# A two-layer graph attention kernel: where the second layer's tiles live and are cleared, how the first layer's last groups are drained, and how the last four norms are ordered

## The chip, the core and the metric

The kernel runs on one core of a Trainium2 chip. Its engines work side by side, each through its own instructions in the order written: PE (matmul; weight loads, PEld, run beside it), DVE (vector), ACT (scalar functions and copies), POOL (GpSimd, which also issues the gathers) and SP (here only a queue for transfers). The metric is device time in microseconds, lower is better. Time before: 877.46 us, the median of three runs (876.76 to 881.76).

## The reference

Eight graphs share one adjacency of 2048 nodes. x is (8, 2048, 64).

```
mask = adj + eye(N) > 0
h   = einsum('bnc,hdc->bhnd', x, Wh)                  # 4 heads of 64
out = softmax(where(mask, h h^T, -1e16)) h + bh
z   = leaky_relu(concat over heads, 0.2)
h2  = einsum('bnk,dk->bnd', z, Wo)
z2  = leaky_relu(softmax(where(mask, h2 h2^T, -1e16)) h2 + bo, 0.2)
y   = (z2 - mean) * rsqrt(var + 1e-5) * gamma + beta
result = layernorm(x + y)
```

So each node passes two norms at the end: the layer's own (with gamma and beta), then, after the residual, a second one.

## The kernel before, in words

The adjacency is sparse but for 56 dense "hub" nodes. The other 1992 nodes are put in 166 sets of 12. For each set the program lists at most 128 neighbours, and a gather on POOL (L792) fetches their rows for all eight graphs, 260 KB, from a table in memory: table1 holds x, table2 holds the first layer's output.

Tiles come from pools. `const` lives through the whole program. `early`, `rowp` and `work` serve the first layer and are released together after it. `late` is opened after that and serves the second layer, in the same memory. The order of instructions on each engine is the order in which the program writes them.

**First layer.** A loop over i from -4 to 85 works on groups of two sets (83 groups). In iteration i, in program order: scores of group i+1 on PE and their mask on DVE (L826); projection of group i-1 on PE into a PSUM tile `cat` (tag C, two banks), copied by ACT (L518, z); ACT copies xTg and takes the exponential; values of group i on PE, reciprocal and scaling on DVE (L853, L854, osb); two gathers; DVE's leaky step (L523); then for group i-2 the second layer's map on PE (L880) into `cat`, for group i-3 a transpose (L890) into `cat`; columns of i+4 into `cat`; DVE copies the map (L885, own) and adds the bias to the transposed rows (L894, rowt), which two transfers on SP store to table2 (L897); picking jobs on DVE; ACT's copy y (L812) and, after PE's transposes, its copy otb (L870), which the next projection needs. PSUM tags S, T, O and C have one buffer each, so a new tile of a tag waits for the readers of the last one. The last iterations (83 to 85) only drain groups.

**Between the layers** the first 24 gathers from table2 are issued on POOL, and DVE clears the tiles of the second layer (L1107 to L1117): `ownb` (the hubs' own columns, block-wise), three `bd` (the sets' own columns, block-wise, refilled by ACT in `spread_own`, L1124), two `es2` (weights), two `esh` (hub weights), and `linked` (a byte mask). They are `late` tiles.

**Second layer.** A loop over steps u from -4 to 48 takes four sets a step (42 steps with sets): scores of u+2 (PE, exponential on ACT), values of u, gathers of u+6, hub blocks for some steps, `roots(u)` (logarithm and exponential on ACT, which make 1/sqrt of the variances gathered in a batch), `spread_own(u+3)`, transposed scores of u+1 and their mask on DVE (L1152), transposes of u+4 with ACT copies (L1320). Every second step ends a block of 8 sets, and `norm` hands back its jobs, which are laid into later steps: for a norm that begins in step v, each step has a first and a second slot.

- v, second slot: scale by the softmax sum, leaky step, row sums (L1186 to L1197)
- v+1, first: centre on DVE (L1202), square on ACT (L1204)
- v+2, first: variance on DVE (L1213), into a batch whose root is taken in step v+2
- v+3, second: scale (L1217), times gamma (L1221), plus residual xr (L1222), row sums
- v+4, first: centre, square; v+6, first: variance; v+7, first: scale and store

Eight transfers store a norm's rows (L1248), all on SP, but for the last norm, where four go on the ACT queue. There are 21 such norms (v = 1, 3, ... 41) and one for the hubs.

Of the kernel before, what the change touches and what calls it, by code (L numbers as in the profile page):

```python
# [359 lines left out]
def fast_kernel(ctx: ExitStack, tc: tile.TileContext, x, adj, Wh, bh, Wo, bo, gamma, beta, out, flag):  # L360
# [51 lines left out]
    make_identity(nc, ident)  # L412
    identb = const.tile([P, P], BF16, name="identb")
    nc.vector.tensor_copy(identb, ident)
    wnat = early.tile([P, H, C], F32, name="wnat")
    whT = early.tile([P, H * D], F32, name="whT")
    gram = early.tile([P, H, P], F32, name="gram")
    wos = early.tile([D, H * D], F32, name="wos")
# [68 lines left out]
    number = early.tile([P, 2, HALFN], U16, name="number")  # L487
# [81 lines left out]
    yh = early.tile([P, 2, 2 * HUB * H], F32, name="yh")  # L569

    def hub_columns():
        py = two("pyh")
# [87 lines left out]
    hub_osb = {}  # L660


    keys = [early.tile([P, HALFN], F32, name=f"keys{k}") for k in range(2)]
    cand = early.tile([P, SEG * KEEP], F32, name="cand")
    best = early.tile([P, P], F32, name="best")
    ahead = {}
    byset = adj[HUB:, :].rearrange("(k s) m -> k s m", s=NS)

# [223 lines left out]
    def keep_rows(g, pr):  # L892
        r = rowts[g % 4]
        nc.vector.tensor_tensor(r[:GM, 1:1 + P], pr, bob[:GM].rearrange("n p d -> n (p d)"), OP.add)  # L894
# [115 lines left out]
    def late_two(name):  # L1010
        return one(name, "T")

    picks = pick(1)
    ready, done = FIRST, 2 * FIRST
    todo3 = [(10, 0), (14, 1)]
    slow = hub_later(0, one) + hub_later(1, one)
    for i in range(-4, NG + 3):
        if 0 <= i + 1 < NG:
            sp = one(f"s{i + 1}", "S")
            scores(i + 1, sp)  # L1020
            weigh(i + 1, sp)
        if i >= 1 and slow and len(slow) % 3:
            slow.pop(0)()
        cat = one(f"cat{i}", "C")
        if 0 <= i - 1 < NG:
            project(held.pop(("ot", i - 1)), cat, GM)
            held["z", i - 1] = leaky(cat, GM, f"z{i - 1}")
        if 0 <= i + 2 < NG:
            t = held["T", 1, i + 2] = work.tile([P, 2, 512], F32, tag="xTg", name=f"xTg{i + 2}", bufs=3)
            nc.scalar.copy(t, held.pop(("tp", i + 2)))  # L1030
        if 0 <= i + 1 < NG:
            lift(i + 1)
        if 0 <= i < NG:
            op = one(f"o{i}", "O")
            values(i, op)
            invert(i, op)
        if 0 <= i + LOOK < NG and i > -3:
            for j in range(2):
                gather(table1, 2 * (i + LOOK) + j, 1, rows_tile)
        if i + 6 < NG and i % 2 == 0 and i >= -2:  # L1040
            own_rows((i + 6) // 2)
        if 0 <= (i - 30) // 2 <= NV:
            (add_beta if i % 2 else load_own)((i - 30) // 2)
        if 0 <= i - 1 < NG:
            leak(held["z", i - 1])
        if i >= 0:
            if turns():
                some(1)
            if slow and len(slow) % 3 == 0:
                slow.pop(0)()  # L1050
            more(1)
            if todo3 and i == todo3[0][0]:
                make_keys(2, todo3.pop(0)[1], late_two)
            if not picks:
                ready = done
            if not picks and not todo3 and done < NS:
                picks = pick(2)
                done = NS
            assert i + 1 + LOOK >= NG or 2 * (i + 1 + LOOK) + 1 < ready

        if 0 <= i - 2 < NG:
            second_maps(i - 2, cat[:, 0, 384:384 + GM])
        if 0 <= i - 3 < NG:
            second_rows(i - 3, cat[:GM, 1, 384:512])
        if 0 <= i + 4 < NG + NG % 2:
            columns(i + 4, cat)
        if 0 <= i - 2 < NG:
            keep_own(i - 2, cat[:, 0, 384:384 + GM])
        if 0 <= i - 3 < NG:
            keep_rows(i - 3, cat[:GM, 1, 384:512])  # L1070
        for _ in range((2 if i < 22 or i % 2 else 1) if i >= 0 else 0):
            if not turns():
                some(1)
        if 0 <= i + 4 < NG + NG % 2:
            keep_columns(i + 4, cat)
        if 0 <= i + 3 < NG:
            tp = held["tp", i + 3] = one(f"t{i + 3}", "T")
            turn(tp[:, 0, :], rows[1, 2 * (i + 3)])
        if 0 <= i < NG:
            turn_values(i, op)  # L1080
            keep_values(i, op)
        if 0 <= i + 3 < NG:
            turn(tp[:, 1, :], rows[1, 2 * (i + 3) + 1])
    assert not picks and not pieces and not todo3 and done == NS
    begin.close()
    stage.close()

# [7 lines left out]
    def rows2(name):  # L1095
        return late.tile([P, Q, PW], F32, tag="rows", name=name, bufs=24)

    NU = (NS + 3) // 4
    sets = [list(range(4 * u, min(4 * u + 4, NS))) for u in range(NU)]
    for u in range(6):  # L1100
        for s in sets[u]:
            gather(table2, s, 2, rows2)
    bd = [late.tile([P, 4, Q, 32], F32, name=f"bd{k}", bufs=1) for k in range(3)]
    es2 = [late.tile([P, 2 * Q, 4, 32], F32, name=f"es2_{k}", bufs=1) for k in range(2)]
    esh = [late.tile([P, Q * 2 * HUB + 8], F32, name=f"esh{k}", bufs=1) for k in range(2)]
    ownb = late.tile([P, Q, 2, HUB], F32, name="ownb", bufs=1)
    nc.vector.memset(ownb, 0.0)  # L1107
    for p in range(2):
        nc.vector.tensor_copy(ownb[half(p), :, p, :], ownh[half(p)].rearrange("c t (k n) -> c (t k) n", k=2))
    for t in bd:  # L1110
        nc.vector.memset(t, 0.0)
    for k in range(2):
        nc.vector.memset(esh[k][:, Q * 2 * HUB:], 1.0)
        nc.vector.memset(es2[k], 0.0)
    nc.vector.memset(es2[0][:, :, :, 24:], 1.0)
    linked = late.tile([P, NS, SET], U8, name="linked", bufs=1)
    nc.vector.tensor_scalar(linked, mask.rearrange("p s (k h) -> p s k h", h=H)[:, :, :, 0], 0.0, None, OP.is_equal)  # L1117

    def spread_own(u):

        w = len(sets[u])
        for p in range(2):
            src = own[half(p), :, sets[u][0] * SET:(sets[u][0] + w) * SET]
            nc.scalar.copy(bd[u % 3][half(p), :w, :, 16 * p:16 * p + SET], src.rearrange("c q (k n) -> c k q n", k=w))  # L1124

    def scores2(u):

# [43 lines left out]
    def norm(name, v, i, vals, dens, nb, store):  # L1171

        y = late.tile([P, 8, D], F32, tag="y", name=f"y_{name}", bufs=6)[:, :nb]
        st = late.tile([P, 2, 8], F32, tag="st", name=f"st_{name}", bufs=6)[:, :, :nb]
        at = [v + 2, v + 6]
        xr = late.tile([P, 8, D], F32, tag="xr", name=f"xr_{name}", bufs=3)
        nc.sync.dma_start(out=xr.rearrange("p b d -> p (b d)"), in_=table3[i])
        row = lambda t: t.unsqueeze(1).to_broadcast([P, nb, D])
# [27 lines left out]

        def var(k):
            def job():
                if at[k] not in batches:
                    batches[at[k]] = late.tile([P, 2, 8], F32, tag="var", name=f"var{at[k]}", bufs=6), []  # L1210
                t, used = batches[at[k]]
                used.append((k, nb))
                nc.vector.tensor_reduce(t[:, k, :nb], sqs.pop(k), AX.X, OP.add)  # L1213
            return job

        def scale(k):
            nc.vector.tensor_tensor(y, y, col(batches[at[k]][0][:, k, :nb]), OP.mult)  # L1217
# [12 lines left out]

    def roots(u):

        if u not in batches:
            return
        t, used = batches[u]
        flat = t.rearrange("p a b -> p (a b)")
        parts = [flat] if used == [(0, 8), (1, 8)] or used == [(1, 8), (0, 8)] else [t[:, k, :nb] for k, nb in used]
        for v in parts:
            nc.scalar.activation(v, v, AF.Ln, bias=shifts[:, 2:3], scale=1.0 / D)
            nc.scalar.activation(v, v, AF.Exp, scale=-0.5)  # L1240

    def norm_sets(v, op):
        def store(y):
            for t in range(4):
                for a in range(2):
                    dst, w = nodes(t, v)(out, a)
                    p0 = t * 32 + a * SET
                    (nc.scalar if v == NV - 1 and a else nc.sync).dma_start(out=dst, in_=y[p0:p0 + SET].rearrange("p (f w) c -> p f (w c)", f=2)[:, :, :w * D])  # L1248
# [98 lines left out]
    assert len(hub_at) == NHB + 1  # L1347
    for b in range(4):
        hub_block(b)
    spread_own(0)  # L1350
    for u in range(-4, NU + 7):
        if 0 <= u + 2 < NU:
            scores2(u + 2)
# [80 lines left out]
```

## Time and profile before

| | |
|---|---|
| median of three runs | 877.46 us |
| profiled execution, its own time | 880.76 us |
| its span, first to last instruction | 878.9 us |
| PE busy | 753.0 us (86%) |
| DVE busy | 610.1 us (69%) |
| ACT busy | 514.4 us (59%) |
| POOL busy | 469.2 us (53%) |
| mean granted PE clock | 0.951 |

The page cuts the span into 40 slices of 22 us; each digit is a slice's busy share in tenths. "Idle before, releaser" in a row says how long the engine stood before an instruction and whose end let it go. Rows in order of time carry start and duration in us. The first layer's loop runs from about 150 to 600 us, the second layer from about 605 us to the end.

### The profile page before, as it was taken

How to read it: one execution, taken by the hardware profiler on the slowest of the kernel's cores; microseconds unless marked ns; L12 is line 12 of the kernel's file. 1: busy time of each engine (PE TensorE's matmuls, PEld its weight loads, DVE VectorE, ACT ScalarE, POOL GpSimd, SP SyncE). 2: the span in 40 equal slices, each digit the busy share in tenths (PEclk: the TensorE clock that was granted, in tenths of full speed). 3: DMA queues.
4: the chain of work that ended last, by engine and by line, in shares of the span. 5: the costliest groups of instructions: out<-in, count | busy, mean ns of one | idle time of the engine just before them, and what ended most of it. 6: DMA issues, size and time to landing. Idle time of an engine off the chain costs nothing.

```text
span 878.9 us, 42066 instructions
## 1 busy us (share of the span) xinstructions
PE 753.0 (86%) x18437; PEld 661.2 (75%) x18437; DVE 610.1 (69%) x1369; ACT 514.4 (59%) x961; POOL 469.2 (53%) x612
## 2 busy tenths in 40 slices
PE   1896777889999999999999999992999999998730
PEld 1664456778788999988999999971899999988720
DVE  3356983568888788877555555553258999998994
ACT  2342333556556667666766667651678888886821
POOL 5654141457444555655666666503777777777300
PEclk9998998999999999999999999995999999999965
DMA  8787451355434445655566665514888888888611
GB/s 167 238 218 213 129 146 48 83 142 160 109 100 118 112 125 159 162 169 153 160 168 173 160 166 162 134 28 114 246 266 253 275 275 267 266 252 242 172 46 35
DMA packets 81794, 145.22 MB, mean 165 GB/s; under 512 B 30146, under 2 KB 46466, under 8 KB 81602
## 3 DMA queue, kind: packets, MB, share of 16 engines
q0 software_dynamic: 26720, 88.55, 36.4%
q1 hardware_dynamic: 37842, 49.65, 18.7%
q10 hardware_dynamic: 17040, 4.25, 2.6%
q8 instruction: 147, 2.41, 1.1%
q14 instruction: 45, 0.37, 0.1%
HBM read 123.91 MB, written 18.48 MB: 162 GB/s over the span
## 4 chain that ended last, share of the span: by engine, by line
PE 63%; DVE 15%; DMA 7%; ACT 5%; issue 4%; SPq 3%; POOL 2%; DVEq 0%; ACTq 0%; POOLq 0%
PE t L512 11%; PE s L821 10%; PE o L846 10%; PE cat L806 6%; PE o L863 4%; PE cat L531 4%; PE cat L880 3%; PE s L1133 3%; PE o L1165 3%; PE cat L890 2%; DMA raw<-in_adj_dram 2%; SPq L1248 2%; PE sh L1277 2%; PE e L1144 2%; DMA g<-table,index 1%
## 5 line engine op out<-in xcount | busy, mean ns | idle before, releaser
L792 POOL DMA_INDIRECT g<-table,index x332 | 334.9, 1009 | 236.1 <-PE o L846 140.2
L512 PE MATMUL t<-ident,g 128*128 128x128 f32 x1328 | 182.3, 276 | 15.6 <-DMA g<-table,index 12.7
L512 PEld LDWEIGHTS t<-ident,g 128*128 128x128 f32 x1328 | 154.8, 142 | 20.0 <-issue 14.0
L826 DVE TENSOR_TENSOR e<-s,mask 128x768 f32<-128x768 f32 x83 | 79.4, 956 | 87.4 <-PE s L821 85.4
L518 ACT ACTIVATE z<-cat,bhp 128x192 f32<-128x192 f32 x166 | 60.8, 418 | 85.0 <-PE cat L531 85.0
L846 PE MATMUL o<-g,e 128*64 128x65 f32 x2656 | 97.5, 227 | 0.0
L821 PEld LDWEIGHTS s<-y,xTg 64*64 64x64 f32 x5312 | 85.2, 134 | 13.9 <-issue 13.7
L821 PE MATMUL s<-y,xTg 64*64 64x48 f32 x5312 | 95.5, 220 | 0.0
L846 PEld LDWEIGHTS o<-g,e 128*64 128x64 f32 x2656 | 85.8, 140 | 9.8
L1320 ACT COPY xTg<-t 128x1024 f32<-128x1024 f32 x83 | 80.3, 1017 | 18.1 <-PE t L512 17.3
L1030 ACT COPY xTg<-t 128x1024 f32<-128x1024 f32 x83 | 84.0, 1012 | 2.0 <-PE t L512 2.0
L833 ACT ACTIVATE e<-e,shifts 128x768 f32<-128x768 f32 x83 | 79.2, 955 | 2.1 <-DVE e L826 1.7
L812 ACT COPY y<-cat 128x384 f32<-128x384 f32 (+1 forms) x80 | 40.7, 508 | 64.0 <-PE o L863 40.1
L597 ACT ACTIVATE e<-e,shifts 128x896 f32<-128x896 f32 x32 | 33.4, 1042 | 73.0 <-DVE e L594 52.1
L680 POOL TENSOR_SCALAR a<-raw 120x1024 bf16<-120x1024 int32 (+1 forms) x34 | 38.2, 1125 | 65.1 <-DMA raw<-in_adj_dram 38.4
L806 PE MATMUL cat<-xo,gram 128*128 128x192 f32 (+1 forms) x320 | 65.6, 328 | 0.0
L853 DVE RECIPROCAL rall<-o 64x8 f32<-64x8 f32 x166 | 34.0, 205 | 42.0 <-PE o L846 40.7
L854 DVE TENSOR_TENSOR osb<-o,rall 128x512 f32<-128x512 f32 x83 | 57.4, 692 | 2.9
L1165 PE MATMUL o<-g,es 128*32 128x65 f32 x2656 | 49.1, 226 | 5.9 <-DVE y_s L1188 4.5
L806 PEld LDWEIGHTS cat<-xo,gram 128*128 128x128 f32 x320 | 53.7, 203 | 0.3 <-issue 0.2
L1165 PEld LDWEIGHTS o<-g,es 128*32 128x32 f32 x2656 | 46.1, 113 | 7.0 <-issue 4.9
L1133 PE MATMUL s<-xTg,bd 128*32 128x128 f32 x1328 | 45.4, 277 | 6.2 <-ACT bd L1124 3.5
(177 smaller groups left out, 1369.3 us busy)
## 6 DMA issues: line engine op xcount, KB each, us to landing
raw<-in_adj_dram SPq DMA_DIRECT2D x32, 480.0 KB
table<-xb SPq DMA_DIRECT2D x22, 256.0 KB
xr_s<-table SPq DMA_DIRECT2D x21, 256.0 KB
g<-table,index POOLq DMA_INDIRECT x332
table<-x SPq DMA_DIRECT2D x16, 260.0 KB
x<-in_x_dram ACTq DMA_DIRECT2D x32, 128.0 KB
table<-rowt SPq DMA_DIRECT2D x166, 24.4 KB
xb<-in_x_dram SPq DMA_DIRECT2D x164, 24.0 KB
```

The lines of the kernel that those rows point to most:

```text
L512: nc.tensor.transpose(tp[:, q * P:(q + 1) * P], rows[:, q, 1:1 + P], ident)
L518: nc.scalar.activation(z[:, hp], cat[:, :, hp * n:(hp + 1) * n], AF.Identity, bias=bhp[:, hp:hp + 1], scale=1.0)
L792: nc.gpsimd.indirect_dma_start(out=t.rearrange("n q c -> n (q c)"), out_offset=None, in_=table, in_offset=bass.IndirectOffsetOnAxis(ap=ind ...
L806: nc.tensor.matmul(cat[:, k, 2 * GM:2 * GM + n], gram[:, g % 2 * 2 + k, :], held["x", g // 2][:, :n], start=True, stop=True)
L821: nc.tensor.matmul(sp[half(r), p, (q * 2 + j) * M:(q * 2 + j + 1) * M], xt[half(p), j, q, half(r)], y[half(p), (j * Q + q) * M:(j * Q + q ...
L826: nc.vector.tensor_tensor(e[:, :16 * M].rearrange("p (a q n) -> p a q n", a=2, q=Q), sp[:, :, :8 * M].rearrange("p a (q n) -> p a q n", q= ...
L833: nc.scalar.activation(e[:, :16 * M], e[:, :16 * M], AF.Exp, bias=shifts[:, 0:1], scale=1.0)
L846: nc.tensor.matmul(op[half(p), j, o0:o0 + K1], e[:, c0:c0 + 64], rw[j][:, q, sums(p)], start=True, stop=True)
L1030: nc.scalar.copy(t, held.pop(("tp", i + 2)))
L1133: nc.tensor.matmul(sp[q * 32:(q + 1) * 32, k, :], bd[u % 3][:, k, q, :], xt[:, s % 2, q, :], start=True, stop=True, tile_position=(0, q * 32))
L1165: nc.tensor.matmul(op[t * 32:(t + 1) * 32, f, k * W2 + p:k * W2 + p + K1], e[:, 2 * q + p, k, :], rw[:, q, sums(p)], start=(a == 0 and k = ...
L1320: nc.scalar.copy(t, tp)
```

## The change

The second layer's tiles are no longer taken from `late`. Six tiles `share` in `const` serve early helpers first (weights, keys, candidate lists, index numbers, hub columns) and the second layer afterwards; `linked` lies in a part of `maskh`. Their clears, and the first three `spread_own`, are jobs that the first layer's loop takes up one at a time, in odd iterations from 61 to 81. In iterations from 83 on the map and the transpose of a group get tiles of tags S and T instead of a part of `cat`. For the last two groups the second row store goes on the ACT queue. For the last four set norms (v = 35, 37, 39, 41) eight steps become three, and for the first three of them gamma and residual are computed on POOL. Roots are batched apart for these norms, and the last norm's eight stores are spread over SP, ACT and POOL.

```diff
-    wnat = early.tile([P, H, C], F32, name="wnat")
+    share = [const.tile([P, n], F32, name=f"share{k}") for k, n in enumerate([HALFN, HALFN, HALFN, 512, 512, 2 * 456])]
+    wnat = share[3][:, :H * C].rearrange("p (h c) -> p h c", h=H)
...
-    keys = [early.tile([P, HALFN], F32, name=f"keys{k}") for k in range(2)]
+    keys = share[:2]
...
-            nc.sync.dma_start(out=dst[2 * g + j], in_=r[j * 48:(j + 1) * 48])
+            (nc.scalar if j and g >= NG - 2 else nc.sync).dma_start(out=dst[2 * g + j], in_=r[j * 48:(j + 1) * 48])
...
+    bd = [t.rearrange("p (k q n) -> p k q n", k=4, q=Q) for t in (share[2][:, :512], share[2][:, 512:], share[4])]
+    es2 = [t.rearrange("p (b k n) -> p b k n", b=2 * Q, k=4) for t in share[:2]]
+    esh = [share[5][:, k * 456:(k + 1) * 456] for k in range(2)]
+    ownb = share[3][:, :Q * 2 * HUB].rearrange("c (q p n) -> c q p n", q=Q, p=2)
+    linked = maskh[:, 1:10, :].rearrange("p m n -> p (m n)")[:, :NS * SET].rearrange("p (s k) -> p s k", k=SET)
...
+    def clear_own():
+        nc.vector.memset(ownb, 0.0)
+        for p in range(2):
+            nc.vector.tensor_copy(ownb[half(p), :, p, :], ownh[half(p)].rearrange("c t (k n) -> c (t k) n", k=2))
+
+    def clear_ends():
+        for k in range(2):
+            nc.vector.memset(esh[k][:, Q * 2 * HUB:], 1.0)
+        nc.vector.memset(es2[0][:, :, :, 24:], 1.0)
+
+    def link():
+        nc.vector.tensor_scalar(linked, mask.rearrange("p s (k h) -> p s k h", h=H)[:, :, :, 0], 0.0, None, OP.is_equal)
+
+    ahead_of_second = ([clear_own] + [lambda t=t: nc.vector.memset(t, 0.0) for t in bd + es2] + [clear_ends, link] +
+                       [lambda u=u: spread_own(u) for u in range(3)])
...
-        cat = one(f"cat{i}", "C")
+        cat = one(f"cat{i}", "C") if i <= NG else None
+        if i < NG:
+            ph, pr = cat[:, 0, 384:384 + GM], cat[:GM, 1, 384:512]
+        else:
+            ph, pr = one(f"ph{i}", "S")[:, 0, :GM], one(f"pr{i}", "T")[:GM, 0, :P]
...
+        if i >= 60 and i % 2 and ahead_of_second:
+            ahead_of_second.pop(0)()
...
-        at = [v + 2, v + 6]
+        quick = 2 * NV - 7 <= v < 2 * NV and nb == 8
+        at = [v + 1, v + 2] if quick else [v + 2, v + 6]
...
         def again():
             scale(0)
-            nc.vector.tensor_tensor(y, y, row(gam), OP.mult)
-            nc.vector.tensor_tensor(y, y, xr[:, :nb], OP.add)
+            eng = nc.gpsimd if quick and v < 2 * NV - 1 else nc.vector
+            eng.tensor_tensor(y, y, row(gam), OP.mult)
+            eng.tensor_tensor(y, y, xr[:, :nb], OP.add)
...
+        if quick:
+            return [([], [first, act, mean(0), centre(0)]), ([var(0)], [again, mean(1), centre(1)]), ([var(1)], [end])]
         return [([], [first, act, mean(0)]), ([centre(0)], []), ([var(0)], []), ([], [again, mean(1)]), ([centre(1)], []),
                 ([], []), ([var(1)], []), ([end], [])]
...
-                    (nc.scalar if v == NV - 1 and a else nc.sync).dma_start(out=dst, in_=y[p0:p0 + SET].rearrange("p (f w) c -> p f (w c)", f=2)[:, :, :w * D])
+                    queue = nc.sync if v < NV - 1 else (nc.sync, nc.scalar, nc.gpsimd)[(2 * t + a) % 3]
+                    queue.dma_start(out=dst, in_=y[p0:p0 + SET].rearrange("p (f w) c -> p f (w c)", f=2)[:, :, :w * D])
...
-        if 0 <= u + 3 < NU and u > -3:
+        if 3 <= u + 3 < NU:
             spread_own(u + 3)
```

In these lines NG is 83, NV 21, NU 42, NS 166 and HALFN 1024. The deleted allocations and clears of the second layer, which stood where `late` is opened, and the renaming of the batches of roots are left out.

More of the change, by code (lines that the diff above doesn't have):

```diff
@@ L414, in fast_kernel @@
     nc.vector.tensor_copy(identb, ident)
-    wnat = early.tile([P, H, C], F32, name="wnat")
+    share = [const.tile([P, n], F32, name=f"share{k}") for k, n in enumerate([HALFN, HALFN, HALFN, 512, 512, 2 * 456])]
+    wnat = share[3][:, :H * C].rearrange("p (h c) -> p h c", h=H)
     whT = early.tile([P, H * D], F32, name="whT")
     gram = early.tile([P, H, P], F32, name="gram")
-    wos = early.tile([D, H * D], F32, name="wos")
+    wos = share[3][:D, H * C:H * C + H * D]
     woT = early.tile([P, HP, D], F32, name="woT")
@@ L486, in fast_kernel @@
                                 compare_op=OP.not_equal, fill=float(1 << k))
-    number = early.tile([P, 2, HALFN], U16, name="number")
+    number = share[2].bitcast(U16).rearrange("p (h c) -> p h c", h=2)
     nc.gpsimd.iota(number, [[1, 2], [2, SEG // 2], [SEG, HALFN // (SEG // 2)]], base=0, channel_multiplier=0)
@@ L567, in hub_mask_sets @@
                                     pm[:np_, b0 // 9, b0 % 9 * HUB:(b0 % 9 + n) * HUB], 0.0, 255.0, OP.is_equal, OP.mult)
-    yh = early.tile([P, 2, 2 * HUB * H], F32, name="yh")
+    yh = share[5][:, :4 * HUB * H].rearrange("p (t n) -> p t n", t=2)
     def hub_columns():
@@ L660, in fast_kernel @@
     hub_osb = {}
-    keys = [early.tile([P, HALFN], F32, name=f"keys{k}") for k in range(2)]
-    cand = early.tile([P, SEG * KEEP], F32, name="cand")
-    best = early.tile([P, P], F32, name="best")
+    keys = share[:2]
+    cand = share[4][:, :SEG * KEEP]
+    best = share[4][:, SEG * KEEP:SEG * KEEP + P]
     ahead = {}
@@ L1011, in late_two, with spread_own @@
         return one(name, "T")
+    NU = (NS + 3) // 4
+    sets = [list(range(4 * u, min(4 * u + 4, NS))) for u in range(NU)]
+    bd = [t.rearrange("p (k q n) -> p k q n", k=4, q=Q) for t in (share[2][:, :512], share[2][:, 512:], share[4])]
[3 more added lines that the diff above has]
+    linked = maskh[:, 1:10, :].rearrange("p m n -> p (m n)")[:, :NS * SET].rearrange("p (s k) -> p s k", k=SET)
+    def spread_own(u):
+        w = len(sets[u])
+        for p in range(2):
+            src = own[half(p), :, sets[u][0] * SET:(sets[u][0] + w) * SET]
+            nc.scalar.copy(bd[u % 3][half(p), :w, :, 16 * p:16 * p + SET], src.rearrange("c q (k n) -> c k q n", k=w))
+    def clear_own():
+        nc.vector.memset(ownb, 0.0)
+        for p in range(2):
+            nc.vector.tensor_copy(ownb[half(p), :, p, :], ownh[half(p)].rearrange("c t (k n) -> c (t k) n", k=2))
[7 more added lines that the diff above has]
+                       [lambda u=u: spread_own(u) for u in range(3)])
     picks = pick(1)
@@ L1061, in fast_kernel @@
         if 0 <= i - 2 < NG:
-            second_maps(i - 2, cat[:, 0, 384:384 + GM])
+            second_maps(i - 2, ph)
         if 0 <= i - 3 < NG:
-            second_rows(i - 3, cat[:GM, 1, 384:512])
+            second_rows(i - 3, pr)
         if 0 <= i + 4 < NG + NG % 2:
@@ L1067, in fast_kernel @@
         if 0 <= i - 2 < NG:
-            keep_own(i - 2, cat[:, 0, 384:384 + GM])
+            keep_own(i - 2, ph)
         if 0 <= i - 3 < NG:
-            keep_rows(i - 3, cat[:GM, 1, 384:512])
+            keep_rows(i - 3, pr)
         for _ in range((2 if i < 22 or i % 2 else 1) if i >= 0 else 0):
@@ L1083, in fast_kernel @@
             turn(tp[:, 1, :], rows[1, 2 * (i + 3) + 1])
-    assert not picks and not pieces and not todo3 and done == NS
+    assert not picks and not pieces and not todo3 and done == NS and not ahead_of_second
     begin.close()
@@ L1096, in rows2 @@
         return late.tile([P, Q, PW], F32, tag="rows", name=name, bufs=24)
-    NU = (NS + 3) // 4
-    sets = [list(range(4 * u, min(4 * u + 4, NS))) for u in range(NU)]
     for u in range(6):
@@ L1102, in fast_kernel @@
             gather(table2, s, 2, rows2)
[L1103 to L1124, printed above, removed]
     def scores2(u):
@@ L1208, in job @@
             def job():
-                if at[k] not in batches:
-                    batches[at[k]] = late.tile([P, 2, 8], F32, tag="var", name=f"var{at[k]}", bufs=6), []
-                t, used = batches[at[k]]
+                if (at[k], quick) not in batches:
+                    batches[at[k], quick] = late.tile([P, 2, 8], F32, tag="var", name=f"var{at[k]}_{quick}", bufs=6), []
+                t, used = batches[at[k], quick]
                 used.append((k, nb))
@@ L1216, in scale @@
         def scale(k):
-            nc.vector.tensor_tensor(y, y, col(batches[at[k]][0][:, k, :nb]), OP.mult)
+            nc.vector.tensor_tensor(y, y, col(batches[at[k], quick][0][:, k, :nb]), OP.mult)
         def again():
             scale(0)
-            nc.vector.tensor_tensor(y, y, row(gam), OP.mult)
-            nc.vector.tensor_tensor(y, y, xr[:, :nb], OP.add)
+            eng = nc.gpsimd if quick and v < 2 * NV - 1 else nc.vector
+            eng.tensor_tensor(y, y, row(gam), OP.mult)
+            eng.tensor_tensor(y, y, xr[:, :nb], OP.add)
         def end():
@@ L1231, in roots, with root @@
     def roots(u):
-        if u not in batches:
-            return
-        t, used = batches[u]
+        for quick in range(2):
+            if (u, quick) in batches:
+                root(*batches[u, quick])
+    def root(t, used):
         flat = t.rearrange("p a b -> p (a b)")
@@ L1349, in fast_kernel @@
         hub_block(b)
-    spread_own(0)
     for u in range(-4, NU + 7):
```

## The prediction

> **What bounds the kernel now.** I read the slices first, then the stretches of 10 us at the end, then the instructions in order of time at the three places that the change touches.
>
> ```profile
> PE   1896777889999999999999999992999999998730
> DVE  3356983568888788877555555553258999998994
> 840.00:850.00 10.00, 3.68 (x98) 2.89 (x98) 9.66 (x19) 1.75 (x4) 0.00 (x0) 0.66 0.23 58
> 850.00:860.00 10.00, 0.19 (x2) 0.09 (x2) 9.46 (x22) 1.87 (x5) 0.00 (x0) 0.50 0.13 34
> 860.00:870.00 10.00, 0.00 (x0) 0.00 (x0) 6.98 (x11) 2.54 (x8) 0.00 (x0) 0.50 0.18 36
> ```
>
> The columns after the stretch are busy us of PE, PE's loads, DVE, ACT, POOL. PE sets the pace of both layers (9s), with one hole of some 16 us between them and a tail from about 835 us in which DVE alone is busy, 9.5 of 10 us. So three prices decide: PE's pace in the late first layer, the hole, and the queue of DVE in the tail.
>
> Late first layer (start, duration, engine):
>
> ```profile
> 479.05 0.55 DVE L523 SCALAR_TENSOR_TENSOR z<-z 128x384 f32<-128x384 f32 x1
> 479.68 0.28 DVE L894 TENSOR_TENSOR rowt<-cat,bob 96x128 f32<-96x128 f32 x1
> 480.05 0.51 ACT L812 COPY y<-cat 128x384 f32<-128x384 f32 x1 [0.66 <-PE o L863]
> 480.43 0.54 ACT L870 COPY otb<-o 128x192 f32<-128x192 f32 x2
> 481.32 0.53 PE L531 MATMUL cat<-otb,whT 64*64 64x96 f32 x16
> 393.57 0.28 DVE L894 TENSOR_TENSOR rowt<-cat,bob 96x128 f32<-96x128 f32 x1
> 393.94 0.52 ACT L812 COPY y<-cat 128x384 f32<-128x384 f32 x1 [1.57 <-DVE rowt L894]
> ```
>
> The last two rows are an iteration in which DVE was late: ACT's y copy started 0.09 us after rowt ended, so it waits for rowt. otb follows y on ACT and PE's projection needs otb. In the usual iteration otb ends at 480.97 and PE comes to the projection at 481.32: the cover is 0.3 us.
>
> The hole and the end:
>
> ```profile
> 605.05 0.43 DVE L1107 MEMSET ownb<- 128x448 f32 x1 [4.36 <-DMA table<-rowt]
> 605.49 0.96 POOL L792 DMA_INDIRECT g<-table,index  x1 [5.56 <-DVE ownb L1107]
> 611.09 1.08 PE L512 MATMUL t<-ident,g 128*128 128x128 f32 x4 [10.73 <-DMA g<-table,index]
> 867.57 7.38 SPq L1248 DMA_DIRECT2D out_dram<-y_s  x12
> 868.74 0.69 DVE L1217 TENSOR_TENSOR y_s<-y_s,var 128x512 f32<-128x512 f32 x1 [0.61 <-ACT var L1240]
> ```
>
> ```profile
> L928 POOL TENSOR_TENSOR xb<-xb,bet x22: 1273/1282/1298, 338.3 to 551.0; 128x512 f32<-128x512 f32 x22
> ```
>
> The hole is a chain: last row of table2, its landing, first gather, its landing. At the end SP still issues stores after the last DVE instruction. The row by itself, from the view of the tile xb (duration in ns, least, median, most), prices a two-input 128x512 operation on POOL: 1.28 us.
>
> Moving tiles between pools issues nothing.
>
> **Part 1, the clears inside the first layer.** Eight DVE jobs land in odd iterations 61 to 75, after osb and before leak. DVE runs from osb to rowt without a gap, so a job of length d moves rowt, y and otb by d, and PE stands for d - 0.3. From the rows of the hole: own clear and copies 1.03, three bd clears 0.52 each, two es clears 0.91, ends 0.57 with the gaps, linked 1.20. Stalls: 0.7 + 3 x 0.2 + 2 x 0.6 + 0.3 + 0.9 = 3.7, and PE is fully busy there (20.0 of 20 us), so I put +3.8 with rounding up for hops. Bounds: 0 if otb is not held, +6.2 (all the d) if there is no cover. The three spreads are 0.7 us each on ACT, in front of the y copy, in an idle time of 0.66: nothing; uncovered they cost 2.1.
>
> **Part 2, the drain.** The rows of the last groups no longer share PSUM tile C with the z copies. PE's matmul for group 82 started at 597.95 behind rowt of group 80; with tiles S and T (last readers at 587.0 and 583.7) it can start when keep_own of 81 ends, about 597.3: -0.65, and the last row is ready at 600.04 instead of 600.69. SP issued the last four stores back to back, 599.82 to 602.02, at 0.58 each; with two of them on the ACT queue the last issue starts when its row is ready and ends at about 600.65. Behind these issues ACT has nothing to do until 614.5. Landing (2.04) stays. Together -1.4.
>
> **Part 3, the hole.** After landing at 604.11 POOL spends 0.75 us on queue waits until 604.8, yet the gather starts when the ownb memset ends (605.48). Whether POOL waits for it the trace does not say: 0 to -0.6, I take -0.3. Later, ACT's spread at 624.01 (0.70) stood between the esh exponential and the xTg copy for which PE waited: -0.7; the one at 629.11 lay beside PE's transposes: 0. Linked (1.20) stretched one gather from 1.25 to 2.10, but PE waited only for the first three: 0, at best -0.85. The two bd and the two esh buffers now share a tile; if a whole tile is guarded, DVE's second hub score (621.82) would wait for PE's first hub values (until 623.42): up to +1.6, taken as 0, since later in the layer the reader stands ahead anyway. The second layer is then PE-paced (19.5 of 20 us), so the shift carries to the tail. Parts 2 and 3: -2.4, bounds +0.9 to -4.2, and about 0 if landing is limited by DMA (share 0.95 from 610 to 615).
>
> **Part 4, the four short norms** (a step is one pass u of the second layer's loop; they begin in steps 35, 37, 39, 41, step 35 at 820.4). DVE is in order and its instructions are written as listed: scale, then on POOL times gamma and plus residual, then mean. Nothing of DVE stands between, so DVE idles for the pair: 0.07 + 1.28 + 0.02 + 1.28 + 0.07 = 2.72. Three norms: +8.2; removed are six DVE instructions at 0.72 spacing (856.52, 857.25, 857.97): -4.3. Net +3.9. No gather is behind the POOL pair: the last was issued at 822.8.
> The old eight steps also filled ACT's round trips with other norms' work. A trip centre, square, variance leaves DVE 0.80 idle (865.04 to 866.45, less its own 0.60); variance, ln, exp, scale leaves 0.68 (867.46 to 868.74, less 0.60). Going through the new order, squares are bare twice (second of 39 and 41) and covered but for 0.2 three times: 2.2. Roots: first of 39 0.3, first of 41 0.7; second of 35 0.7 and of 37 0.6 (an older norm's root is now separate, 0.5 more on ACT), of 39 and 41 0.7 each: 3.7. The square also stands ahead of the next exponential on ACT, which holds the transposed scores: about 0.65 in steps 36 and 38: 1.3. Sum 7.2; such idles that fall away now: 0.62 + 1.13 + 0.61 = 2.4. Net +4.8. DVE in the tail: +8.7, bounds +0.5 (pair hidden) and +11.
> The SBUF — State Buffer page of the Trainium skill (Who interferes with whom) says that a DVE instruction with two SBUF inputs and a GpSimd instruction that reads SBUF exclude each other. The trace has a cousin of it:
>
> ```profile
> 399.35 1.87 DVE L777 TENSOR_SCALAR mask<-member 128x672 uint8<-128x672 int32 x1
> 399.56 1.28 POOL L928 TENSOR_TENSOR xb<-xb,bet 128x512 f32<-128x512 f32 x1
> ```
>
> The DVE row takes 0.51 us elsewhere; here it ended only after POOL's. By my order DVE stands anyway, so the page adds nothing to the sum; in the rival where DVE works beside POOL it would take back most of the gain. The GPSIMD Engine Reference (Elementwise, side-by-side) gives POOL 1.96 times DVE's time for a two-input operation; an estimate from that page is 1.35 instead of 1.28 per operation, +0.4 on the sum.
>
> **Part 5, the last stores.** From the last DVE end (869.43) to the span's end 9.5 us pass: SP issues until 874.95, because norm 39's eight stores are ahead of norm 41's, then 2.0 landing and 1.9 closing. Now norm 39 stores over 10 us earlier and the last eight are split 3, 3, 2. SP's three at 0.41 give 1.3; POOL's two, bounded by a gather's 1.25, 2.5. So 5.2 to 6.4 remain: -3.7, bounds -2.4 and -4.3.
>
> **Sum.** 3.8 - 2.4 + 8.7 - 3.7 = +6.4. The profiled execution took 880.76 us (span 878.9), 3.3 above the median of 877.46; its own time would be 887.2, and a median 883.9.
>
> **Rivals.**
> A: the sum, 883.9, its own range 878 to 888.
> B, faster: the tail is bound by the length of the last chain (850.8 to 869.4, 18.6 us through seven steps), so closing it up pays, and DVE finds work while POOL runs; the clears hide too. -4.3 + 4.8 - 3.7 - 2.4 = -5.6: 871.9. For it: the three idles before scale. Against: DVE 9.5 of 10 busy until 860. It decides if DVE's idle in steps 36, 38 and 40 stays under 1 us each.
> C, slower: the clears have no cover (+6.2) and the drain gives only 0.7: 6.2 - 0.7 + 8.7 - 3.1 = +11.1: 888.6. For it: DVE's rows touch from osb to rowt.
> D: the hole does not do what the change says, because hub blocks and gathers fill the DMA (0.95): 2.4 less gained, 886.3. Against: the first gather's own 5.6 us follow its start.
>
> **Chances.** A 0.62, B 0.15, C 0.13, D 0.10. About 1% (8.8 us) can be told from no change: 868.7 and 886.2. Slower: C, half of D and a fifth of A, 0.30. Faster: a third of B and a little, 0.06. Same: 0.64. 875 to 890 leaves out most of B and the upper half of C, 0.19.
>
> **What would show it.** Right: PE's projections at odd iterations 61 to 75 come late by 0.2 to 0.9 us; the first layer-2 gather starts about 2 us sooner after the last projection; DVE idles 2.7 us with POOL as releaser in steps 36, 38, 40; only eight stores follow the last scale. Wrong: DVE's tail ends no later relative to the start of step 35, or PE keeps 5.00 us an iteration through the clears.

## The result, and the profile after

The changed kernel takes 887.85 us (median of 9 runs, 883.51 to 893.23) against 879.59 us for the kernel before on the same chip (9 runs, 876.76 to 888.12). The ratio is 1.009, interval 1.0063 to 1.0116: about 1% slower. (Of all runs told of here one, in experiment 9, fell into a slower state; ratios leave it out.) The profiled execution took 887.44 us, its span 885.7 us, 6.8 more than before.

From the page of the changed kernel, then its stretches at the end (columns as before: length, busy us of PE, PE's loads, DVE, ACT, POOL):

```profile
PE   2886778889989999999999899993999999998640
DVE  3346873668888778876555666651268998999865
```

```profile
830.00:840.00 10.00, 4.27 (x111) 3.94 (x110) 6.82 (x12) 4.34 (x8) 2.52 (x2) 0.88 0.23 53
840.00:850.00 10.00, 6.97 (x187) 5.94 (x185) 6.39 (x12) 3.96 (x10) 2.52 (x2) 0.78 0.30 66
850.00:860.00 10.00, 3.90 (x78) 2.96 (x82) 8.66 (x16) 2.95 (x9) 0.02 (x1) 0.57 0.13 28
860.00:870.00 10.00, 0.89 (x32) 0.65 (x24) 5.75 (x10) 1.19 (x4) 2.52 (x2) 0.50 0.24 52
870.00:880.00 10.00, 0.19 (x2) 0.09 (x2) 7.19 (x16) 2.28 (x6) 0.12 (x1) 0.50 0.07 13
```

DVE has POOL's 2.52 us off its list in three stretches, and yet finishes later: in the tail it is busy 6 to 9 of 10 us, where it had been 9.5 to 9.8 up to 860 us. What it waits for stands in the rows in order of time (start, duration; idle before and its releaser in brackets):

```profile
833.12 1.26 POOL L1237 TENSOR_TENSOR y_s<-y_s,gam 128x512 f32<-128x512 f32 x1 [8.22 <-DVE y_s L1232]
834.46 1.26 POOL L1238 TENSOR_TENSOR y_s<-y_s,xr_s 128x512 f32<-128x512 f32 x1
835.76 0.69 DVE L1212 TENSOR_REDUCE st_s<-y_s 128x8 f32<-128x512 f32 x1 [2.72 <-POOL y_s L1238]
...
850.06 0.69 DVE L1212 TENSOR_REDUCE st_s<-y_s 128x8 f32<-128x512 f32 x1 [2.73 <-POOL y_s L1238]
...
863.50 0.69 DVE L1212 TENSOR_REDUCE st_s<-y_s 128x8 f32<-128x512 f32 x1 [2.72 <-POOL y_s L1238]
865.60 0.69 DVE L1228 TENSOR_REDUCE var_True<-sq_s 128x8 f32<-128x512 f32 x1 [0.69 <-ACT sq_s L1219]
866.90 0.69 DVE L1232 TENSOR_TENSOR y_s<-y_s,var_True 128x512 f32<-128x512 f32 x1 [0.61 <-ACT var_True L1261]
...
879.62 1.38 SPq L1270 DMA_DIRECT2D out_dram<-y_s  x3
879.62 1.24 ACTq L1270 DMA_DIRECT2D out_dram<-y_s  x3
879.88 1.28 POOL L1270 DMA_DIRECT2D out_dram<-y_s  x2 [16.42 <-DVE y_s L1232]
```

Three times DVE stands 2.7 us for POOL's pair; then the round trips over ACT are bare (0.69 for the square, 0.61 for the root). After the last scale only eight stores are left.

In the first layer the costly place is iteration 61, which takes `clear_own`:

```profile
488.08 0.43 DVE L1030 MEMSET share<- 128x448 f32 x1
488.55 2.14 DVE L1032 COPY share<-ownh 64x224 f32<-64x224 f32 x2
489.26 1.28 POOL L929 TENSOR_TENSOR xb<-xb,bet 128x512 f32<-128x512 f32 x1
490.72 0.56 DVE L524 SCALAR_TENSOR_TENSOR z<-z 128x384 f32<-128x384 f32 x1
491.37 0.28 DVE L895 TENSOR_TENSOR rowt<-cat,bob 96x128 f32<-96x128 f32 x1
491.73 0.51 ACT L813 COPY y<-cat 128x384 f32<-128x384 f32 x1 [3.43 <-DVE rowt L895]
492.12 0.54 ACT L871 COPY otb<-o 128x192 f32<-128x192 f32 x2
492.72 0.78 PE L532 MATMUL cat<-otb,whT 64*64 64x96 f32 x16 [2.31 <-ACT otb L871]
```

The chain is the one of the prediction (rowt, y, otb, projection), but PE stands 2.31 us, not 0.7: the two copies took 2.14 us and ended at 490.69, 0.15 after POOL's addition. And the hole between the layers:

```profile
603.84 0.29 DVE L895 TENSOR_TENSOR rowt<-pr,bob 96x128 f32<-96x128 f32 x1 [0.54 <-PE pr L891]
607.79 0.96 POOL L793 DMA_INDIRECT g<-table,index  x1 [4.50 <-DMA table<-rowt]
611.95 0.87 PE L513 MATMUL t<-ident,g 128*128 128x128 f32 x3 [8.15 <-DMA g<-table,index]
```

No clear stands ahead of the first gather now; POOL waits for the landing of the rows.

I cut both spans at marks that every trace has: the first and last projection of the first layer (P1, P2), the first scores of the second layer (S), the start of step 35, the last DVE end. All in us, from one profiled execution each, the last columns for variants that the next section tells of:

| stretch | before | after | old norms | clears back | norms all on DVE |
|---|---|---|---|---|---|
| start to P1 | 162.5 | 162.8 | 161.0 | 167.3 | 165.0 |
| P1 to P2 (loop) | 432.6 | 436.9 | 438.2 | 429.9 | 435.8 |
| P2 to S (hole) | 26.7 | 24.9 | 25.3 | 25.5 | 25.0 |
| S to step 35 | 198.7 | 197.1 | 197.9 | 197.5 | 197.3 |
| step 35 to last DVE end (tail) | 49.0 | 58.0 | 49.0 | 57.6 | 54.1 |
| to the span's end | 9.5 | 6.1 | 8.8 | 6.4 | 6.2 |

"Start of step 35" is DVE's first variance of that step (820.40 before, 821.55 after). The start differs by up to 8 us from execution to execution, and so do transfers early in the loop; therefore single stretches, and the last 25 iterations of the loop, carry more than whole spans. Those 25 took 123.7 us before, 129.4 after.

### The profile page after: what moved, and what is told of

The parts are those of the page before. It is cut to its first block, busy times and chain, and to the rows that moved or that the text cites. A ratio compares the mean times of both kernels' runs of the same rounds, so it can differ in the third digit from the quotient of the medians.

```text
span 885.7 us, 42092 instructions
## 1 busy us (share of the span) xinstructions
PE 757.0 (85%) x18437; PEld 663.6 (75%) x18437; DVE 609.0 (69%) x1363; ACT 515.7 (58%) x969; POOL 481.2 (54%) x620
## 4 chain that ended last, share of the span: by engine, by line
PE 66%; DVE 13%; issue 6%; ACT 6%; DMA 5%; POOL 2%; SPq 1%; ACTq 0%; POOLq 0%; DVEq 0%
PE t L513 13%; PE o L847 9%; PE s L822 9%; PE cat L807 6%; PE cat L532 4%; PE s L1147 3%; PE o L864 3%; PE o L1179 3%; PE cat L881 3%; PE e L1158 2%; PE cat L891 2%; PE sh L1299 2%; ACT xTg L1342 2%; DVE e L595 1%; DMA x<-in_x_dram 1%
## 5 line engine op out<-in xcount | busy, mean ns | idle before, releaser
L513 PE MATMUL t<-ident,g 128*128 128x128 f32 x1328 | 184.2, 278 | 13.8 <-DMA g<-table,index 11.1
L513 PEld LDWEIGHTS t<-ident,g 128*128 128x128 f32 x1328 | 157.0, 144 | 17.9 <-issue 11.4
L1179 PE MATMUL o<-g,share 128*32 128x65 f32 x2656 | 49.3, 228 | 4.6 <-DVE y_s L1203 3.4
L532 PE MATMUL cat<-otb,whT 64*64 64x96 f32 x1328 | 45.0, 249 | 8.2 <-ACT otb L871 5.5
L595 DVE TENSOR_TENSOR e<-sh,maskh 128x896 f32<-128x896 f32 x32 | 34.8, 1087 | 24.0 <-PE sh L591 21.2
```

The source lines that it names most:

```text
L513: nc.tensor.transpose(tp[:, q * P:(q + 1) * P], rows[:, q, 1:1 + P], ident)
L532: nc.tensor.matmul(cat[half(j), s, hp * n:(hp + 1) * n], whT[half(s), h * D:(h + 1) * D], ot[half(s), h, :], start=True, stop=True)
L1179: nc.tensor.matmul(op[t * 32:(t + 1) * 32, f, k * W2 + p:k * W2 + p + K1], e[:, 2 * q + p, k, :], rw[:, q, sums(p)], start=(a == 0 and k = ...
```

## The experiments

Eleven kernels. The first four are the changed kernel with one thing undone or moved. The kernel before had a median of 879.64 us beside them (28 runs).

**1. The old order of the norms, all else as changed.**

```diff
-        quick = 2 * NV - 7 <= v < 2 * NV and nb == 8
+        quick = False
```

> The changed kernel with all norms in the old eight steps and nothing on GpSimd but the gathers; clears, drain and the three store queues stay as changed. My theory (the short norms cost the tail 9.0 us on DVE and save 3.4 us of stores): from the start of step 35 to the last DVE end 49 us instead of 58.0, then about 9 us instead of 6.1; in all 6 us less than the changed kernel, about 881.8 against 887.8, a ratio to before of 1.002 to 1.004. Rival (the tail grew because it starts from another state after the moved clears): 58 us stay, no change against the changed kernel.

Measured: 881.47 us, ratio 1.0031 (1.0008 to 1.0054). The tail is back at 49.0 us and the closing stretch is 8.8. So the norms and their stores carry 0.6 of the 0.9%, and the rest, clears and drain together, is still slower than nothing.

**2. The clears back between the layers.** They run behind the first 24 gathers, on the new tiles.

```diff
-        if i >= 60 and i % 2 and ahead_of_second:
-            ahead_of_second.pop(0)()
...
+    while ahead_of_second:
+        ahead_of_second.pop(0)()
```

> The changed kernel with the eleven jobs (clears, mask, three spreads) run between the layers, behind the first 24 gathers in program order. My theory (the clears stall PE through rowt, y and otb): the iterations 61 to 76 go back to 5.00 us, 6 us less, the first gather comes up to 0.6 us later after the last projection and the first steps of the second layer up to 1 us later: 4.5 us less in all, about 883.3, a ratio of 1.004. Rival (the long iterations have another cause, such as an instruction fetch, and the clears are hidden): 0 to 2 us more than the changed kernel.

Measured: 884.28 us, ratio 1.005 (1.0021 to 1.0079). The last 25 iterations took 122.3 us instead of 129.4: the clears cost 7.1 us there. The hole is 25.5 instead of 24.9. These 0.6 us can't be put down to the clears: experiment 5, which has them between the layers too, has 24.9. The new tiles are free before the first layer ends, so DVE begins to clear them while the rows land (the copies at 602.00, the first gather at 605.20) and the gather waits for the rows alone. The shorter hole belongs to the drain and the new tiles; clearing inside the loop was not needed for it.

**3. Gamma and residual of the short norms on DVE.**

```diff
-            eng = nc.gpsimd if quick and v < 2 * NV - 1 else nc.vector
+            eng = nc.vector
```

> The changed kernel with gamma and residual of the short norms on DVE; their order stays. My theory: three stops of 2.72 us for the POOL pair become three pairs of 1.44 us, 3.9 us less, about 884.0; the bare round trips to ACT stay and keep the tail from step 35 at 54 us, 5 above before. Rival (only the round trips cost, the POOL pair is as long as DVE's own work): within 1 us of the changed kernel. Other rival (the POOL pair is the whole loss): 49 us.

Measured: 884.27 us, ratio 1.0051 (1.0023 to 1.0078). The tail is 54.1: 4.0 less than with GpSimd, 5.0 more than in the old order. That splits the tail's loss into the pair on GpSimd and the closing up itself.

**4. `clear_own`'s two copies on ACT.** The theory: they stand because POOL adds beside them. The rival: any instruction of DVE at this place costs PE so much.

```diff
-            nc.vector.tensor_copy(ownb[half(p), :, p, :], ownh[half(p)].rearrange("c t (k n) -> c (t k) n", k=2))
+            nc.scalar.copy(ownb[half(p), :, p, :], ownh[half(p)].rearrange("c t (k n) -> c (t k) n", k=2))
```

> The changed kernel with the two copies of the first job (hub columns into ownb) on ACT instead of DVE. My theory (in iteration 61 the DVE copies stood for POOL's two-input addition, took 2.14 instead of 0.57 us, and PE's clock fell behind the stop): iteration 61 takes 5.0 to 5.9 us instead of 7.49, the next 5.0 instead of 6.55, 3 to 4 us less, about 884.3. Rival (the copies are slow wherever they run or the stop has another cause): iteration 61 stays above 7 us.

Measured: 886.08 us, ratio 1.0068 (1.0036 to 1.0101). In order of time in this kernel:

```profile
489.62 0.43 DVE L1030 MEMSET share<- 128x448 f32 x1
490.09 0.77 ACT L1032 COPY share<-ownh 64x224 f32<-64x224 f32 x2 [0.25 <-DVE share L1030]
490.54 0.28 DVE L895 TENSOR_TENSOR rowt<-cat,bob 96x128 f32<-96x128 f32 x1
491.31 1.28 POOL L929 TENSOR_TENSOR xb<-xb,bet 128x512 f32<-128x512 f32 x1
491.32 0.54 ACT L871 COPY otb<-o 128x192 f32<-128x192 f32 x2
491.91 0.56 PE L532 MATMUL cat<-otb,whT 64*64 64x96 f32 x16
```

The iteration takes 5.14 us where it took 7.49, the next 5.04 where it took 6.55; the last 25 sum to 125.7 instead of 129.4. The rows say what the theory says, and DVE's memset at the same place now costs 0.14 us, which speaks against the rival. The whole time shows only 1.8 of these 3.6 us, and I can't tell that from the spread.

The next four were measured beside 878.9 us for the kernel before (35 runs). They look for a version that keeps what is good in the change; all have the old order of norms.

**5. The new drain and the last norm's stores only** (experiments 1 and 2 in one).

> Of the change only the drain (tiles of tags S and T, two row stores on ACT's queue) and the split of the last stores remain; clears between the layers, old norms. My theory: the first second-layer scores come 1.2 us sooner after the last projection than before (25.5 against 26.7 us), the stores give 0.7, the rest is as before: about 877.7 against 879.6, a ratio of 0.998. Rival (the shared tiles cost something in the second layer by themselves): 880 or more, with more than 198.7 us from the first scores to the start of step 35.

Measured: 879.45 us, ratio 1.0007 (0.9988 to 1.0026). The hole is 24.9 us and the tail 49.0, so the stretch of the hole is 1.8 better than before and the closing stretch 0.7 (8.7), but the whole time doesn't show it: the expected 0.998 lies below the interval. From S to step 35 it took 197.7 us, so the rival's sign (more than 198.7) isn't there either.

**6. The clears in the loop again, but in even iterations and behind the rows,** after the picking jobs.

```diff
+        if i >= 60 and i % 2 == 0 and ahead_of_second:
+            ahead_of_second.pop(0)()
         if 0 <= i + 4 < NG + NG % 2:
             keep_columns(i + 4, cat)
```

> Old norms; the eleven jobs stay in the first layer, but in even iterations (no addition of beta on GpSimd there) and behind the row additions, so that rowt, y and otb do not wait for them. My theory (the cost of the clears is their place ahead of rowt, and GpSimd's addition): every iteration from 60 on takes 5.00 to 5.05 us, and the gain of the hole (0.6 us) and of the drain is kept: about 877, a ratio of 0.997. Rival (any clear there costs PE its length): iterations of 5.2 to 5.9 us as in the changed kernel, about 881.

Measured: 877.51 us, ratio 0.9978 (0.9953 to 1.0003). All iterations from 60 on, up to the shorter last five, take 4.99 to 5.00 us, but for one of 5.28, where the kernel before has one of 5.57; the last 25 sum to 122.5 (122.3 in experiment 2). The same clears cost nothing when y and otb don't wait for them. Two things were moved at once, place and iterations; experiment 11 moves the iterations alone, and there the other jobs keep their cost, so it is the place.

```profile
489.51 0.28 DVE L895 TENSOR_TENSOR rowt<-cat,bob 96x128 f32<-96x128 f32 x1
489.83 0.43 DVE L1030 MEMSET share<- 128x448 f32 x1
490.27 0.55 ACT L871 COPY otb<-o 128x192 f32<-128x192 f32 x2
490.30 0.92 DVE L1032 COPY share<-ownh 64x224 f32<-64x224 f32 x2
491.15 0.53 PE L532 MATMUL cat<-otb,whT 64*64 64x96 f32 x16
```

These are the rows of `clear_own` here. The copies take 0.92, and the projection starts 5.00 after the last one (486.16) all the same.

**7. GpSimd's pair spread out.** Experiment 6, with gamma and residual of the norms v = 33 to 39 on GpSimd, and the second mean and centre two steps later, so that DVE has other work while POOL runs. This is the way that the faster rival of the prediction would need.

```diff
+        pooled = 33 <= v < 41 and nb == 8
...
+            eng = nc.gpsimd if pooled else nc.vector
...
+        if pooled:
+            return [([], [first, act, mean(0)]), ([centre(0)], []), ([var(0)], []), ([], [again]), ([], []),
+                    ([mean(1), centre(1)], []), ([var(1)], []), ([end], [])]
```

> As y2, and gamma and residual of the norms that begin in steps 33 to 39 run on GpSimd, with the mean that needs them two steps later, so that DVE has other norms' work meanwhile. My theory (GpSimd cost because DVE stood for it): no stop of DVE with GpSimd as releaser, and four pairs of 1.43 us less on DVE in the tail: step 35 to the last DVE end 44 to 46 us instead of 49.0, about 873, a ratio of 0.992 to 0.994. Rival (the two engines exclude each other on inputs in SBUF): DVE's two-input rows beside GpSimd's pairs take up to 1.3 us longer and the tail stays at 48 to 50 us.

Measured: 880.7 us, ratio 1.0005 (0.998 to 1.003), the tail 48.5 us instead of 49.0. Missed. DVE no longer stands for POOL anywhere in the tail; it stands for PE, in the steps where PE and ACT still work:

```profile
828.26 0.69 ACT L1150 ACTIVATE eT<-s,shifts 128x512 f32<-128x512 f32 x1
829.00 0.66 PE L1158 MATMUL e<-ident,eT 128*128 128x128 f32 x4 [0.67 <-ACT eT L1150]
829.70 0.56 DVE L1166 TENSOR_TENSOR share<-e,maskh 128x384 f32<-128x384 f32 x1 [2.31 <-PE e L1158]
```

What was taken off DVE before about 840 us came back as waiting for the transposed scores, which come through ACT's exponential and PE: 2.31 and 1.83 us, in steps 37 and 39. Relief is worth something only behind them. The rival is true as well, in part. Beside POOL's pairs two of DVE's two-input rows took longer, 1.00 and 1.48 us instead of 0.69:

```profile
855.93 1.26 POOL L1239 TENSOR_TENSOR y_s<-y_s,xr_s 128x512 f32<-128x512 f32 x1
856.25 1.48 DVE L1233 TENSOR_TENSOR y_s<-y_s,var_False 128x512 f32<-128x512 f32 x1 [0.62 <-ACT var_False L1265]
```

That makes up the account: 5.7 us taken off DVE, 4.1 back as waiting for PE, 1.1 back beside POOL, and 0.5 left.

**8. Experiment 7, with the stores of the last two norms on three queues.**

```diff
-                    queue = nc.sync if v < NV - 1 else (nc.sync, nc.scalar, nc.gpsimd)[(2 * t + a) % 3]
+                    queue = nc.sync if v < NV - 2 else (nc.sync, nc.scalar, nc.gpsimd)[(2 * t + a) % 3]
```

> As y3, with the stores of the last two norms over three queues instead of the last alone. My theory (what remains behind the last DVE end is SP's backlog from the norm before): from the last DVE end to the end of the span 6.1 to 6.5 us instead of 8.8, about 871, a ratio of 0.990. Rival (landing sets it): 8 us or more.

Measured: 877.86 us, ratio 0.9983 (0.9959 to 1.0007). Missed. The closing stretch falls from 8.8 to 7.2 us, less than expected, and the tail grows from 48.5 to 49.7: stores on ACT's queue stand ahead of a root, and a scale waits 1.29 for it.

The last three stood beside 880.01 us (23 runs).

**9. Experiment 6, with a third of the last but one norm's stores on GpSimd's queue.**

```diff
+                    queue = {NV - 2: (nc.sync, nc.gpsimd, nc.sync), NV - 1: (nc.sync, nc.scalar, nc.gpsimd)}.get(v, (nc.sync,) * 3)[(2 * t + a) % 3]
```

> As y2 (old norms, clears behind the rows in even iterations), and the stores of the second last norm go two thirds to SP and one third to GpSimd's queue, not to ACT's. My theory (SP's backlog is what remains at the end, and stores on ACT's queue stand ahead of a root): from the last DVE end to the end of the span 6.1 to 6.8 us instead of 8.9, the tail from step 35 to the last DVE end stays at 49.0; about 875 against 879, a ratio of 0.9955. Rival: no change against y2, 0.998.

Measured: 877.18 us, ratio 0.9958 (0.9928 to 0.9988). The closing stretch did not shrink (8.85): SP issued until 867.5, 7 us sooner than in experiment 6 (874.6), relative to the last DVE end 2.9 instead of 4.5 us, but 6.0 us then passed to the span's end instead of 4.4. That SP's backlog sets the end is not confirmed; what takes the 6.0 is open. So the ratio came out as expected (0.9955) without the gain that it was expected from: that is luck, and the interval overlaps that of experiment 6.

**10. Experiment 9, with GpSimd's pair for v = 37 and 39 only,** spread out as in experiment 7.

```diff
+        pooled = 37 <= v < 41 and nb == 8
```

> As z1, and gamma and residual on GpSimd only for the norms that begin in steps 37 and 39, where no further transposes wait for ACT. My theory (in y3 the relief of the norms from 33 and 35 ended in DVE waiting for PE's transposed scores, behind ACT's copies; that of the later two counted): step 35 to the last DVE end 46 to 47 us instead of 49.0, a ratio of 0.992 to 0.994. Rival (GpSimd's pairs and DVE hinder each other): 49 us or more.

Measured: 875.79 us, ratio 0.9959 (0.9933 to 0.9985), the tail 47.0. With the norms that end behind PE's last work, each pair on GpSimd takes 1 us off the tail. It is not 1.43, for the same two DVE rows are longer here (1.01 and 1.47 us instead of 0.69): the rival again has its part. The expected ratio was missed, the whole ratio is the same as in experiment 9; 0.7 of the 2.0 us went into the closing stretch (9.55 instead of 8.85), and the rest is seen in the trace and not in the medians. Experiments 9 and 10 are the only ones whose interval lies below 1; the kernel before stood 1.1 us higher beside them than beside experiments 5 to 8.

**11. The changed kernel with its clears in even iterations,** at the place where the change has them, so that `clear_own` doesn't meet POOL's addition. One run.

```diff
-        if i >= 60 and i % 2 and ahead_of_second:
+        if i >= 60 and i % 2 == 0 and ahead_of_second:
```

> The changed kernel with its jobs in even iterations instead of odd ones, at the same place ahead of the leaky step; there GpSimd does a copy of 0.5 us and no two-input addition. My theory: the first job's iteration takes 5.7 to 5.9 us instead of 7.49 and the next one 5.0, the other jobs' iterations keep their 5.2, 5.7 and 5.8 us. Rival (the copies are slow for a reason that has nothing to do with the addition): again above 7 us.

Measured: 889.6 us. The iteration with `clear_own` took 6.43 us, the next 5.03; it was 7.49 and 6.55. The other jobs cost what they did.

```profile
487.41 0.43 DVE L1030 MEMSET share<- 128x448 f32 x1
487.63 0.95 POOL L793 DMA_INDIRECT g<-table,index  x1 [0.30 <-PE cat L807]
487.88 0.80 DVE L1032 COPY share<-ownh 64x224 f32<-64x224 f32 x2
488.59 0.53 POOL L801 COPY xo<-xT 128x192 f32<-128x192 f32 x1
488.70 0.84 DVE L524 SCALAR_TENSOR_TENSOR z<-z 128x384 f32<-128x384 f32 x1
490.99 0.56 PE L532 MATMUL cat<-otb,whT 64*64 64x96 f32 x16 [1.25 <-ACT otb L871]
```

The 2.14 us are gone, as expected of the collision with the addition, but not to the bottom: the copies took 0.80 beside a gather (0.57 before, between the layers), and the leaky step 0.84 (0.56 in iteration 61 above) beside a POOL copy. So the iteration came out above the expected 5.7 to 5.9.

## Why the prediction was right, and where it was not

The likeliest case held: slower, by the sum of four terms. Beside its own base the change cost 8.3 us of median (6.8 in the profiled span) where 6.4 had been forecast. The prediction gave 0.64 to a change that can't be told from none and 0.30 to slower; the interval lies clear of 1. Term by term, from the marks:

| term | predicted | measured | from |
|---|---|---|---|
| clears in the loop | +3.8 | +7.1 | last 25 iterations, after against experiment 2 |
| drain and hole | -2.4 | -1.8 | P2 to S |
| DVE in the tail | +8.7 | +9.0 | step 35 to last DVE end |
| - the pair on GpSimd | +3.9 | +4.0 | after against experiment 3 |
| - the norms closed up | +4.8 | +5.0 | experiment 3 against experiment 1 |
| last stores | -3.7 | -3.4 | last DVE end to the span's end |

The measured terms add up to 10.9, so that the total came out near the forecast is partly luck: what made up for the clears is told below.

**The tail** was right in mechanism and size: stops of 2.72, 2.73 and 2.72 us with POOL as releaser, at the very 2.72 that the durations gave, and the ACT trips bare. The GPSIMD Engine Reference of the Trainium skill (Elementwise, side-by-side) makes POOL 1.96 times as slow as DVE; the rows here make it 1.26 against 0.69, 1.83 times, and the measured row was the better price.

**The stores** and **the drain** were right in the main. The closing 6.1 us lie within the predicted 5.2 to 6.4; the prediction's bound of -2.4 doesn't follow from these (9.5 - 6.4 is 3.1, as in rival C). The first gather comes 8.17 us after the last projection instead of 10.46, 2.3 sooner where 1.7 had been worked out, and 1.8 of it reach the first scores. No part for the clears ahead of the gather is to be seen (experiments 2 and 5). The spread that left ACT's queue was put at -0.7 and gave 0.25: the step after S takes 4.85 us instead of 5.10, in every later trace.

**The clears** are the mis-sized term. The step that failed is "own clear and copies 1.03", a stall of 0.7, priced from the hole, where POOL does no arithmetic. In iteration 61 POOL adds beside them. By line and form the two copies show it:

```profile
L1032 DVE COPY share<-ownh x2: 271/1064/1856, 488.5 to 488.8; 64x224 f32<-64x224 f32 x2
```

The first took 271 ns, the second 1856 (least, median, most). The prediction had a row of this kind, the mask that took 1.87 instead of 0.51, but applied it to the tail only; there DVE stands anyway. The SBUF — State Buffer page of the Trainium skill (Who interferes with whom) says that a DVE copy may use the port pair that it shares with GpSimd, and that whoever is second is then blocked for the whole instruction; the 1856 ns, ending 0.15 us after POOL's addition, agree, and so does their going in experiments 4 and 11. The second copy began at 488.83, though, 0.43 us ahead of the addition and beside a gather that ended at 489.24; the addition followed 0.02 us behind that gather. Beside a gather alone, in experiment 11, it took 515 ns and ended 0.1 us behind it. So here it was most likely held by the gather first, and the addition took over; no run keeps the addition and removes the gather. Of the 7.1 us, 4.0 are this iteration and the next, and without the copies on DVE 3.6 are gone (experiment 4). Two parts make them up: the iteration itself, 2.5 us longer with PE's stop of 2.31, and 1.5 us in the next one, with PE at a lower granted clock. In the stretches of the changed kernel (the third number from the end is the clock):

```profile
487.70:492.70 5.00, 2.71 (x79) 2.39 (x77) 4.69 (x8) 1.53 (x4) 2.78 (x4) 1.00 0.58 167
492.70:494.00 1.30, 1.28 (x26) 1.06 (x28) 0.00 (x0) 0.46 (x2) 0.00 (x0) 0.59 0.17 38
494.00:495.50 1.50, 1.50 (x32) 1.50 (x30) 0.03 (x1) 1.50 (x3) 0.01 (x1) 0.50 0.28 62
495.50:497.00 1.50, 1.50 (x14) 1.26 (x11) 1.45 (x4) 0.51 (x1) 1.20 (x2) 0.72 0.24 58
497.00:499.20 2.20, 2.20 (x73) 2.03 (x75) 0.54 (x3) 0.94 (x3) 1.64 (x3) 1.00 0.76 178
```

For 4.3 us after the stop the clock is 0.50 to 0.72, and the next iteration takes 6.55 instead of 5.00. The other seven jobs cost 3.1 us together where 3.0 had been worked out: iterations of 5.20 for a bd (+0.2, as predicted), 5.73 for an es (+0.7 for 0.6), 5.82 for linked (+0.8 for 0.9), 4.99 for the ends (nothing for 0.3).

**What covered for it.** Against the kernel before the last 25 iterations grew by 5.7 us, not 7.1: its own 123.7 hold an iteration of 5.57 and a last one of 5.10 (granted clock 0.66 from 590 to 595 us), where experiment 2 has 5.00 and 4.17. From S to step 35 the second layer is 1.6 us shorter than before, in the changed kernel and, by 0.8 to 2.3, in all variants. The prediction had left "0, at best -0.85" for linked there. 0.25 of it is the spread told of above; 1.15 come at one place, where PE in the kernel before stands amid the values of a step, for nothing that the profile shows:

```profile
790.81 1.00 PE L1165 MATMUL o<-g,es 128*32 128x65 f32 x56 [0.99 <-issue]
```

No later trace has a stop there; some have one of 0.95 to 1.15 us near the start of the layer (experiments 1, 5 and 9). What causes these stops is open, and with one trace of the kernel before I can't say whether it always has this one. The loop before the last 25 iterations also was 1.4 us shorter in the profiled execution (432.6 - 123.7 = 308.9, against 307.5), within what transfers early in the loop differ by.

**The rivals.** The faster one fell twice. DVE's idle is 2.7, not under 1 us; and when it is arranged that DVE has work meanwhile (experiment 7), the tail gets only 0.5 shorter, for PE's and ACT's chain to the transposed scores takes its place in steps 37 and 39, and POOL's pairs hold up two rows of DVE. The slower one, clears without cover, had the size (+6.2) nearly right, and its 888.6 us lie nearer to the measured 887.85 than the forecast's 883.9 (the base had moved up by 2.1), but it had the reason wrong: the cover of 0.3 us was there for the small jobs, and one collision made up the difference. That the hole would not shrink is refuted by the stretch P2 to S. The predicted addition of 6.4 us is 0.73% of the time, inside the interval of 0.63 to 1.16%.

## What to carry to other kernels

An operation handed to a slower engine relieves the first only if that one has something to do meanwhile in its own order: in three places DVE waited 2.7 us to save 1.4. And the relief counts only where the relieved engine sets the pace (experiments 7 and 10). A filler in a loop goes behind the instruction that the busiest engine waits for; the same clears cost 7 us ahead of the rows and nothing behind them. Ask first whether it needs the loop at all: on tiles that are free early the clears fitted into the wait for the rows (experiments 2 and 5). Price a filler by the neighbour that it will have, not by the quiet place that it comes from.

## What the runs showed of the hardware that was not expected

A DVE copy of 64x224 took 1856 ns instead of 271, to 0.15 us behind GpSimd's two-input addition, and 1848 in both other traces of that order (experiments 1 and 3); beside a gather alone it took 515 (experiment 11), beside a GpSimd copy about 0.63 us (experiment 6). A two-input DVE row of 128x512 took 1.47 and 1.48 us beside the addition instead of 0.69 (experiments 10 and 7), while DVE's sums of squares beside GpSimd's product kept their time (1.27 for two). Memsets on DVE showed nothing of the kind beside gathers (0.91 us for 128x1024, in experiment 6 and the changed kernel alike).

A stop of PE of 2.31 us was followed by 4.3 us at a granted clock of 0.50 to 0.72 in the changed kernel; in experiment 3 the same stop (an iteration of 7.47) was followed by one of 5.03, with the clock at 1.00. Experiment 1 had the low clock again (7.47, then 6.62). What decides it is open.

Stores of results took some 0.6 us each to issue on GpSimd's queue (3.01 for five, experiment 9).
